# Four graph layers in one kernel: one activation table, powers on GpSimd, and relu slots shared by load

## The chip, the cores and the metric

The kernel runs on one core of a Trainium2 chip. Times are device microseconds (us) of one execution. Five engines matter: TensorE (PE, and PEld for its weight loads), VectorE (DVE), ScalarE (ACT), GpSimd (POOL) and the queue that starts transfers.

## The reference, cut to what matters

`x` is 64 batches of 256 nodes with 128 features; `adj` is one 256 x 256 matrix for all of them. Four pre-norm residual layers follow each other:

```python
h = relu(layernorm(x)); x = x + gated_steps(h, adj, 5)      # layer 0, five dependent steps:
#   m = adj @ h;  z = sigmoid(m @ w3' + h @ u3');  r = sigmoid(m @ w4' + h @ u3')
#   hv = tanh(m @ w5' + (r * h) @ u5');  h = (1 - z) * h + z * hv
h = relu(layernorm(x)); x = x + relu(chebyshev_hops(h, adj) @ Theta1 + bias)   # layer 1
h = relu(layernorm(x)); y = (adj @ h + h) @ weight + bias                       # layer 2
x = x + y / maximum(norm(y), 1e-12)
h = relu(layernorm(x))                                                          # layer 3
pre = s1[:, :, None, :] + s2[:, None, :, :] + b_lin      # [batch, i, j, e], e up to 256
e = (where(pre >= 0, pre, 0.2 * pre) * a).sum(-1) + adj
x = x + sigmoid(softmax(e, axis=2) @ h)
```

Layer 3 is the bulk: 256 x 256 x 256 leaky relus for each batch.

## The kernel before

Two batches (a pair) go through all layers together. Of leaky(p) = 0.2 p + 0.8 relu(p) the first part is separable; the second is made by VectorE and ScalarE, [128 e, 256 j] at a time, and summed over e by TensorE with a weight window of 32 columns. A *slot* is one relu tile: eight relus on one engine, then four 32-column products, one for each column group of the array. They run side by side: the four together take 0.86 us, and one alone took 0.97 (both from the trace, in the prediction). A pair has 128 slots.

```python
for r in range(32):
    for k in range(NE):
        rl = relu_pool.tile([P, 4, NB, N], F32, name="rl")        # 6 buffers
        on_act = turn[0] % 3 == 1                                  # every third slot on ScalarE
        turn[0] += 1
        for g in range(4):
            for b in range(NB):
                ...  # nc.scalar.activation(Relu) or nc.vector.tensor_scalar(add, max)
        for g in range(4):
            nc.tensor.matmul(flat[g * 32:(g + 1) * 32, :], win[:, k, 31 - r:63 - r], rl[:, g]...)
    background()          # after two slots: one stage of a softmax tail, one stage of the next pair's front
```

While layer 3 of pair p is worked off, `background()` emits the *front* (layers 0 to 2 and the projections) of pair p + 1. A front stage is mostly a full-width product on TensorE and the step of another engine that takes it out of its PSUM bank:

```python
pm = mix_nodes(h, adj_t, "pm"); mT = feat("mT"); nc.scalar.copy(mT, pm)
yield
pr = project([(w4t, mT), (u3t, hT)], "pr")
pz = project([(w3t, mT), (u3t, hT)], "pz")
nc.scalar.activation(r, pr, AF.Sigmoid, bias=br, scale=1.0)
nc.scalar.activation(z, pz, AF.Sigmoid, bias=bz, scale=1.0)
nc.vector.tensor_mul(rh, r, hT)
yield
pv = project([(w5t, mT), (u5t, rh)], "pv")
nc.scalar.activation(hv, pv, AF.Tanh, bias=bh, scale=1.0)
```

The norms take a square root on ScalarE, for which another activation table has to be loaded (125 of the trace's 285 table loads stand at the two lines of the roots), and a reciprocal on VectorE. The order in which one engine's instructions stand in its queue is decided when the program is built, by the framework's scheduler, from the order of emission and its own estimate of times; the engine then works its queue off in the order that was built.

Of the kernel before, what the change touches and what calls it, by code (L numbers as in the profile page):

```python
# [14 lines left out]
P = 128  # L15
NB = 2  # batches handled together: 512 tokens, one PSUM bank per [128, 512] product
# [3 lines left out]
ALPHA = 0.2  # L20


@with_exitstack
def kernel(
# [22 lines left out]
    """Four pre-norm residual graph layers over x [B, 256, 128].  # L47

    Every batch is independent, so a pair of batches goes through all four
    layers on chip. Token-major tiles are [token % 128, batch, token // 128,  # L50
    feature]; feature-major ones are [feature, batch, token].

    The last layer's scores sum a_e * leaky(s1[i, e] + s2[j, e]) over e. With
    leaky(p) = ALPHA * p + (1 - ALPHA) * relu(p) the first part is separable,
    and the second is relu on the vector and scalar engines (e on partitions,
    j along the free axis, s1[i] as the per-partition scalar), reduced over e
    by the tensor engine: a stationary [128, 32] window, zero but for one
    column that holds (1 - ALPHA) * a, puts row i into its place in PSUM.
    """
# [27 lines left out]
    ident = const.tile([P, P], F32, name="ident")  # L87
    make_identity(nc, ident)
    eps_t = const.tile([P, 1], F32, name="eps_t")
    nc.vector.memset(eps_t, LN_EPS)  # L90

    adj_n = const.tile([P, NC, N], F32, name="adj_n")  # [n, c, m]: adj[c * 128 + n, m]
    nc.sync.dma_start(adj_n, adj.rearrange("(c p) m -> p c m", p=P))
    adj_t = const.tile([P, NC, N], F32, name="adj_t")  # [m, c, n]: adj[n, c * 128 + m]
    adj_ti = const.tile([P, NC, N], F32, name="adj_ti")  # the same of adj + I
# [8 lines left out]
    def load_transposed(w, name):  # L104
        """w [128, D] or [128, 2 * D] -> its transpose, the halves summed (both multiply the same message)."""
        cols = w.shape[1]
        raw = work.tile([P, 2 * D], F32, name="w_raw", bufs=3)
        nc.scalar.dma_start(raw[:, :cols], w)
        src = raw[:, :D]
        if cols == 2 * D:  # L110
            s = work.tile([P, D], F32, name="w_sum")
            nc.vector.tensor_add(s, raw[:, :D], raw[:, D:])
            src = s
        pt = bank([P, P], "pt")
        nc.tensor.transpose(pt, src, ident)
        t = const.tile([P, P], F32, name=name)
        nc.vector.tensor_copy(t, pt)
        return t
# [5 lines left out]
    u5t = load_transposed(u5_w, "u5t")  # L124
# [5 lines left out]
    nc.vector.tensor_add(gate_b[:, 0:1], braw[:, 0:1], braw[:, 3:4])  # L130
    nc.vector.tensor_add(gate_b[:, 1:2], braw[:, 1:2], braw[:, 3:4])
    nc.vector.tensor_add(gate_b[:, 2:3], braw[:, 2:3], braw[:, 4:5])
# [18 lines left out]

    blin = const.tile([P, NE], F32, name="blin")
# [6 lines left out]
    a_lin = const.tile([P, NE, N], F32, name="a_lin")  # L159
    nc.vector.memset(a_lin, ALPHA)  # L160
    for k in range(NE):
        nc.vector.tensor_scalar(win[:, k, 31:32], acol[:, k:k + 1], 1.0 - ALPHA, None, op0=OP.mult)
        nc.vector.tensor_scalar(a_lin[:, k, :], a_lin[:, k, :], acol[:, k:k + 1], None, op0=OP.mult)

# [1 line left out]
    def norm_relu(src, h):  # L166
        """h = relu(layernorm(src)) over the features, token-major."""
# [7 lines left out]
        std = work.tile([P, NB * NC], F32, name="std")  # L175
        nc.scalar.activation(std, mv[:, :, 1], AF.Sqrt, bias=eps_t, scale=1.0)
        rstd = work.tile([P, NB * NC], F32, name="rstd")
        nc.vector.reciprocal(rstd, std)
        for k in range(NB * NC):
            nc.vector.tensor_scalar(hh[:, k, :], s[:, k, :], mv[:, k, 0:1], rstd[:, k:k + 1],  # L180
                                    op0=OP.subtract, op1=OP.mult)
        nc.vector.tensor_scalar(hh, hh, 0.0, None, op0=OP.max)

    def to_feature(h, name):
        """Token-major -> feature-major, in PSUM."""
# [6 lines left out]
    def to_token(ht, name):  # L192
        """Feature-major -> token-major, in PSUM."""
# [6 lines left out]
    def mix_nodes(h, a, name):  # L200
        """[f, b, n] = sum over nodes m of h[b, m, f] * a[m, n], in PSUM."""
# [6 lines left out]
    def project(pairs, name):  # L208
        """[o, b, n] = sum of w[f, o] * t[f, b, n] over the pairs (w, t), in PSUM."""
        pp = bank([P, NB, N], name)  # L210
        for k, (w, t) in enumerate(pairs):
            nc.tensor.matmul(pp.rearrange("p b n -> p (b n)"), w, t.rearrange("p b n -> p (b n)"),  # L212
                             start=(k == 0), stop=(k == len(pairs) - 1))
        return pp

    def project_token(pairs, name):
        """[n, b, c, o] = sum of t[f, b, n] * w[f, o] over the pairs (t, w), in PSUM."""
# [6 lines left out]
        return pp  # L224
# [6 lines left out]

    READY = {}

    def front(p):
        """Layers 0 to 2 of pair p and the operands of layer 3; yields between its stages."""
        x0 = XIN.pop(p)

        # layer 0: gated message passing
        h = tok("h")
        norm_relu(x0, h)  # L240
# [3 lines left out]
        nc.scalar.copy(hT, pt)  # L244
        yield
        for step in range(STEPS):
            pm = mix_nodes(h, adj_t, "pm")
            mT = feat("mT")
            nc.scalar.copy(mT, pm)  # L249
            yield  # L250
            pr = project([(w4t, mT), (u3t, hT)], "pr")
            pz = project([(w3t, mT), (u3t, hT)], "pz")
            r = feat("r")
            nc.scalar.activation(r, pr, AF.Sigmoid, bias=br, scale=1.0)  # L254
            z = feat("z")
            nc.scalar.activation(z, pz, AF.Sigmoid, bias=bz, scale=1.0)  # L256
            rh = feat("rh")
            nc.vector.tensor_mul(rh, r, hT)  # L258
            yield
            pv = project([(w5t, mT), (u5t, rh)], "pv")  # L260
            hv = feat("hv")
            nc.scalar.activation(hv, pv, AF.Tanh, bias=bh, scale=1.0)  # L262
            yield
            # (1 - z) * h + z * hv = h + z * (hv - h)
            nc.vector.tensor_sub(hv, hv, hT)  # L265
            nc.vector.tensor_mul(hv, hv, z)
            hT_new = feat("hT")
            nc.vector.tensor_add(hT_new, hT, hv)
# [3 lines left out]
            if step < STEPS - 1:  # L272
                h = tok("h")
                nc.scalar.copy(h, pt)  # L274
                yield
        x1 = tok("x1")
        nc.vector.tensor_add(x1, x0, pt)
        yield

        # layer 1: Chebyshev hops; both hop families use adj, so their weights are summed  # L280
        h = tok("h")
        norm_relu(x1, h)
# [3 lines left out]
        nc.scalar.copy(hT, pt)  # L286
        yield
        pm = mix_nodes(h, adj_n, "pm")
        c1T = feat("c1T")
        nc.scalar.copy(c1T, pm)  # L290
        yield
        pt = to_token(c1T, "pt")
        c1 = tok("c1")
        nc.scalar.copy(c1, pt)
        yield
        pm = mix_nodes(c1, adj_n, "pm")
        c2T = feat("c2T")
        nc.vector.scalar_tensor_tensor(c2T, pm, 2.0, hT, op0=OP.mult, op1=OP.subtract)
# [3 lines left out]
        for k in range(NB * NC):  # L302
            b, c = divmod(k, NC)
            nc.vector.tensor_add(y[:, b, c, :], po[:, b, c, :], bias1)
        x2 = tok("x2")
        nc.vector.scalar_tensor_tensor(x2, y, 0.0, x1, op0=OP.max, op1=OP.add)
        yield

        # layer 2: (adj + I) h W + bias, rows normalised
        h = tok("h")  # L310
        norm_relu(x2, h)
# [3 lines left out]
        nc.scalar.copy(yT, pm)  # L315
# [3 lines left out]
        for k in range(NB * NC):  # L319
            b, c = divmod(k, NC)  # L320
            nc.vector.tensor_add(y[:, b, c, :], po[:, b, c, :], bias2)
        yield
        sq = tok("sq")
        nc.vector.tensor_mul(sq, y, y)
        nrm = work.tile([P, NB, NC], F32, name="nrm")
        nc.vector.tensor_reduce(nrm, sq, AX.X, OP.add)
        nc.vector.tensor_scalar(nrm, nrm, NORM_EPS * NORM_EPS, None, op0=OP.max)
        nc.scalar.activation(nrm, nrm, AF.Sqrt)
        rn = work.tile([P, NB, NC], F32, name="rn")
        nc.vector.reciprocal(rn, nrm)  # L330
        x3 = tok("x3", bufs=3)
        for b in range(NB):
            for c in range(NC):
                nc.vector.scalar_tensor_tensor(x3[:, b, c, :], y[:, b, c, :], rn[:, b, c:c + 1], x2[:, b, c, :],
                                               op0=OP.mult, op1=OP.add)
        yield

        # layer 3: its input and the two projections by the halves of adj
        h3 = tok("h3", bufs=3)
        norm_relu(x3, h3)  # L340
        yield
        pt = to_feature(h3, "pt")
        hT = feat("hT")
        nc.scalar.copy(hT, pt)
        yield
        s1, s2 = [], []
        for k in range(NE):
            pa = project([(adj_t[:, 0, k * P:(k + 1) * P], hT)], "pa")
            t1 = feat(f"s1_{k}")
            nc.vector.tensor_scalar(t1, pa, blin[:, k:k + 1], None, op0=OP.add)  # L350
            pb = project([(adj_t[:, 1, k * P:(k + 1) * P], hT)], "pb")
            t2 = feat(f"s2_{k}")
            nc.scalar.copy(t2, pb)
# [3 lines left out]
        READY[p] = (x3, h3, s1, s2)  # L357

    def tail(p, ic, pe, x3, h3):
        """Softmax, the weighted sum and the output of rows ic * 128 ... of pair p."""  # L360
        t = work.tile([P, NB, N], F32, name="sc")
        for b in range(NB):
            nc.vector.tensor_add(t[:, b, :], pe[:, b, :], adj_n[:, ic, :])
        nmx = work.tile([P, NB], F32, name="nmx")
        nc.vector.tensor_reduce(nmx, t, AX.X, OP.max, negate=True)  # L365
# [73 lines left out]
    while fronts:  # L439
        step(fronts)  # L440
# [44 lines left out]
```

## Time and profile before

| | before |
|---|---|
| time, median of 3 | 7427.82 us (7427.02 to 7432.16) |
| TensorE, VectorE, ScalarE, GpSimd busy | 98, 92, 75, 0% |
| relus on VectorE / ScalarE | 21848 / 10920 |
| activation table loads | 285, 1283 ns each |
| the chain that ended last | TensorE 87%, VectorE 12% |

The page, the chain and the window sums are shown in the prediction. One more view is the waits (engine, line, what it waited for: us in total, times, longest us). Here are TensorE's weight loads and three of the waits of the relu producers:

```profile
PEld pe L421 <- DVE rl L417: 1569.0, 3674, 2.5
...
ACT rl L415 <- PE pe L421: 394.5, 447, 2.4
DVE rh L258 <- ACT r L254: 237.3, 51, 10.6
...
ACT mT L249 <- PE pm L205: 154.3, 108, 3.9
```

The first line is TensorE waiting for relus of VectorE (counted at its weight loads, which overlap the products before them, so not all of it is lost time). The second is ScalarE waiting for a relu buffer to come free: it has time over. The last two are steps of the front which wait until another engine is done.

### The profile page before, as it was taken

Reading aid. Unit: us, or ns where it says so; the run is one execution under the profiler, and the core shown is the slowest. Engines: PE = TensorE matmul, PEld = TensorE weight load, DVE = VectorE, ACT = ScalarE, POOL = GpSimd, SP = SyncE. Lnnn points to the kernel's source line nnn. Section 1 sums busy time; section 2 is a strip of 40 time slices with the busy share of each in tenths; the row PEclk is TensorE's granted clock in tenths of the full one; section 3 lists DMA queues with packets and bytes.
Section 4 is the critical chain, followed back from the end, with each engine's and each line's share of the span. In section 5 each row is a group of like instructions: output and inputs, shape, how many; then the busy total and the mean of one; then the engine's idle time right before and its main releaser. Section 6 shows DMA issues by size and latency. Waiting matters only on the chain.

```text
span 7427.2 us, 120750 instructions
## 1 busy us (share of the span) xinstructions
PE 7242.1 (98%) x40713; PEld 2490.1 (34%) x40713; DVE 6813.8 (92%) x25298; ACT 5601.2 (75%) x12837; POOL 0.7 (0%) x6
## 2 busy tenths in 40 slices
PE   6999999999999999999999999999999999999999
PEld 3333333333333333333333333333333333333333
DVE  4998999999999999998999999999989999999999
ACT  3777777778777777777777777777877777777777
POOL 0000000000000000000000000000000000000000
PEclk8999999999999999999999999999999999999999
DMA  0000000000000000000000000000000000000000
GB/s 13 3 4 4 3 2 3 4 4 3 2 4 3 4 3 2 4 3 4 4 3 3 3 4 4 3 2 4 3 4 3 2 4 3 4 2 2 2 2 3
DMA packets 38816, 25.83 MB, mean 3 GB/s; under 512 B 3504, under 2 KB 38192, under 8 KB 38192
## 3 DMA queue, kind: packets, MB, share of 16 engines
q1 hardware_dynamic: 35088, 17.05, 0.8%
q8 instruction: 319, 5.23, 0.3%
q14 instruction: 305, 2.50, 0.1%
q10 hardware_dynamic: 3104, 1.05, 0.1%
HBM read 9.70 MB, written 8.39 MB: 2 GB/s over the span
## 4 chain that ended last, share of the span: by engine, by line
PE 87%; DVE 12%; ACT 1%; issue 0%; DMA 0%; SPq 0%; ACTq 0%; DVEq 0%
PE pe L421 58%; PE pm L205 7%; DVE rl L417 6%; PE pr L212 4%; PE pz L212 4%; PE pv L212 4%; PE pe L403 2%; PE pe L399 2%; PE pt L197 2%; DVE h L180 1%; PE po L222 1%; PE po L381 1%; PE pa L212 1%; PE pb L212 1%; DVE stats L173 1%; PE pt L189 1%
## 5 line engine op out<-in xcount | busy, mean ns | idle before, releaser
L417 DVE TENSOR_SCALAR rl<-s,s 128x256 f32<-128x256 f32 x21848 | 5868.7, 347 | 46.8 <-PE pe L421 44.5
L421 PE MATMUL pe<-rl,win 128*32 128x512 f32 x32768 | 5102.9, 599 | 93.4 <-DVE rl L417 93.4
L415 ACT ACTIVATE rl<-s,s 128x256 f32<-128x256 f32 x10920 | 4531.2, 497 | 399.6 <-PE pe L421 394.5
L421 PEld LDWEIGHTS pe<-rl,win 128*32 128x32 f32 x32768 | 1295.7, 109 | 3162.2 <-DVE rl L417 1569.0
L205 PE MATMUL pm<-adj_t,h 128*128 128x256 f32 x1280 | 336.0, 400 | 2.8 <-ACT h L274 2.8
L258 DVE TENSOR_TENSOR rh<-r,hT 128x512 f32<-128x512 f32 x160 | 109.8, 686 | 237.9 <-ACT r L254 237.3
L205 PEld LDWEIGHTS pm<-adj_t,h 128*128 128x128 f32 x1280 | 232.4, 195 | 166.3 <-issue 78.0
L249 ACT COPY mT<-pm 128x512 f32<-128x512 f32 x160 | 93.7, 586 | 155.3 <-PE pm L205 154.3
L254 ACT ACTIVATE r<-pr,gate_b 128x512 f32<-128x512 f32 x160 | 109.9, 687 | 114.5 <-PE pr L212 114.5
L369 ACT ACTIVATE sc<-sc,nmx 128x256 f32<-128x256 f32 x128 | 64.5, 504 | 157.3 <-DVE nmx L365 156.8
L212 PE MATMUL pr<-mT,w4t 128*128 128x512 f32 x320 | 178.9, 641 | 3.5 <-ACT mT L249 3.5
L212 PE MATMUL pv<-mT,w5t 128*128 128x512 f32 x320 | 179.5, 643 | 0.0
L403 PE MATMUL pe<-a_lin,s 128*128 128x256 f32 x512 | 168.6, 419 | 0.0
L212 PE MATMUL pr<-hT,u3t 128*128 128x512 f32 x320 | 167.3, 604 | 0.0
L212 PE MATMUL pz<-mT,w3t 128*128 128x512 f32 x320 | 165.9, 600 | 0.0
L212 PE MATMUL pv<-rh,u5t 128*128 128x512 f32 x320 | 164.5, 595 | 0.0
L262 ACT ACTIVATE hv<-pv,gate_b 128x512 f32<-128x512 f32 x160 | 108.7, 680 | 73.1 <-PE pv L212 73.0
L212 PE MATMUL pz<-hT,u3t 128*128 128x512 f32 x320 | 163.4, 592 | 0.0
L256 ACT ACTIVATE z<-pz,gate_b 128x512 f32<-128x512 f32 x160 | 109.3, 683 | 64.8 <-PE pz L212 64.8
L265 DVE TENSOR_TENSOR hv<-hv,hT 128x512 f32<-128x512 f32 x160 | 109.7, 686 | 37.7 <-ACT hv L262 36.3
L403 PEld LDWEIGHTS pe<-a_lin,s 128*128 128x128 f32 x512 | 80.9, 188 | 181.4 <-issue 179.8
L399 PE MATMUL pe<-s,a_lin 128*128 128x512 f32 x256 | 141.1, 640 | 0.0
(108 smaller groups left out, 3577.9 us busy)
## 6 DMA issues: line engine op xcount, KB each, us to landing
xin<-in_x_dram SPq DMA_DIRECT2D x64, 128.0 KB, 2.2
out_dram<-o SPq DMA_DIRECT2D x64, 128.0 KB, 1.8
w_raw<-in_L_gnn_w_w_dram ACTq DMA_DIRECT2D x3, 128.0 KB, 2.6
th_raw<-in_L_gnn_Theta_dram ACTq DMA_DIRECT2D x1, 320.0 KB, 3.4
adj_n<-in_adj_dram SPq DMA_DIRECT2D x1, 256.0 KB, 4.7
w_raw<-in_L_gnn_u_w_dram ACTq DMA_DIRECT2D x2, 64.0 KB, 2.6
bias<-in_L_gnn_bias_dram ACTq DMA_DIRECT2D x2, 64.0 KB, 3.5
w<-in_L_gnn_weight_dram ACTq DMA_DIRECT2D x1, 64.0 KB, 3.1
```

The source lines that it names most:

```text
L197: nc.tensor.transpose(pt[:, b, c, :], ht[:, b, c * P:(c + 1) * P], ident)
L205: nc.tensor.matmul(pm[:, b, :], h[:, b, c, :], a[:, c, :], start=(c == 0), stop=(c == NC - 1))
L212: nc.tensor.matmul(pp.rearrange("p b n -> p (b n)"), w, t.rearrange("p b n -> p (b n)"), start=(k == 0), stop=(k == len(pairs) - 1))
L254: nc.scalar.activation(r, pr, AF.Sigmoid, bias=br, scale=1.0)
L256: nc.scalar.activation(z, pz, AF.Sigmoid, bias=bz, scale=1.0)
L258: nc.vector.tensor_mul(rh, r, hT)
L265: nc.vector.tensor_sub(hv, hv, hT)
L399: nc.tensor.matmul(flat, a_lin[:, k, :P], s2[k].rearrange("p b n -> p (b n)"), start=(k == 0), stop=False, skip_group_check=True)
L403: nc.tensor.matmul(pe[:, b, :], s1[k][:, b, ic * P:(ic + 1) * P], a_lin[:, k, :], start=False, stop=False, skip_group_check=True)
L415: nc.scalar.activation(rl[:, g, b, :], s2[k][:, b, :], AF.Relu, bias=sc, scale=1.0)
L417: nc.vector.tensor_scalar(rl[:, g, b, :], s2[k][:, b, :], sc, 0.0, op0=OP.add, op1=OP.max)
L421: nc.tensor.matmul(flat[g * 32:(g + 1) * 32, :], win[:, k, 31 - r:63 - r], rl[:, g].rearrange("p b n -> p (b n)"), start=False, stop=(r == ...
```

## The change

Its intent is to unload VectorE and to use ScalarE's free time: one activation table for all (sigmoid(x) = (1 + tanh(x/2))/2; roots as powers on GpSimd), so that table loads go; fewer products (r and z share a bank, the z weights being added as a difference; the separable scores as one product with a vector computed ahead; the second Chebyshev hop as one product with a matrix computed ahead); wider norm passes; each slot given to the engine with the smaller load so far; and a front stage after single slots, spread evenly over the pair. The core of the diff:

```diff
-        nc.scalar.activation(std, mv[:, :, 1], AF.Sqrt, bias=eps_t, scale=1.0)
-        nc.vector.reciprocal(rstd, std)
+        nc.gpsimd.tensor_scalar(dst, src, add, None, op0=OP.add)
+        nc.gpsimd.tensor_tensor(dst, dst, mhalf, op=OP.pow)      # and two stages until it is used
...
-            pr = project([(w4t, mT), (u3t, hT)], "pr")
-            pz = project([(w3t, mT), (u3t, hT)], "pz")
-            nc.scalar.activation(r, pr, AF.Sigmoid, bias=br, scale=1.0)
+            add_project(pg, [(u3t, hT), (w4t, mT)], True, True)
+            act_fn(r, pg, AF.Tanh, br, 0.5)
+            yield
+            add_project(pg, [(w34t, mT)], False, True)           # w34t = w3t - w4t, onto the same bank
...
-            for k in range(NE):      # separable scores: two products of s2, four of s1
-                nc.tensor.matmul(flat, a_lin[:, k, :P], s2[k]...)
-            ...
+            nc.tensor.matmul(pf, v_rep, hT..., start=True, stop=False)
...
-                    on_act = turn[0] % 3 == 1
+                    on_scalar = load["act"] + 8 * 399 < load["dve"] + 8 * 263
...
-                background()         # once per row, that is after two slots
+                    background()     # after each slot
...
-            step(pending)
-            step(fronts)
+            done[0] += 1
+            if done[0] % 4 == 2:
+                step(pending)
+            while fronts and done[1] * (SLOTS - 6) < done[0] * (stages + 1):
+                done[1] += 1
+                step(fronts)
```

## The prediction

> **What bounds the kernel now.** I read the page first (engines, chain of waits, costliest groups), then the chain in order of time inside one pair of batches, then the timeline of TensorE and of two relu stretches. The page:
>
> ```profile
> PE 7242.1 (98%) x40713; PEld 2490.1 (34%) x40713; DVE 6813.8 (92%) x25298; ACT 5601.2 (75%) x12837; POOL 0.7 (0%) x6
> PE 87%; DVE 12%; ACT 1%; issue 0%; DMA 0%; SPq 0%; ACTq 0%; DVEq 0%
> L417 DVE TENSOR_SCALAR rl<-s,s 128x256 f32<-128x256 f32 x21848 | 5868.7, 347 | 46.8 <-PE pe L421 44.5
> L421 PE MATMUL pe<-rl,win 128*32 128x512 f32 x32768 | 5102.9, 599 | 93.4 <-DVE rl L417 93.4
> L415 ACT ACTIVATE rl<-s,s 128x256 f32<-128x256 f32 x10920 | 4531.2, 497 | 399.6 <-PE pe L421 394.5
> ```
>
> Three engines share the relu slots of layer 3: 4096 slots, each of eight relus on VectorE or ScalarE and four 32-column matmuls (two records each) on TensorE. TensorE's 98% cannot be taken at its word, since its ends are modelled. So I price its work from the distance between starts in the chain (start us, us, what):
>
> ```profile
> 3057.22 53.43 PE pe L421 x326
> ...
> 3174.04 0.59 PE pt L197 x4
> 3174.63 1.85 PE pe L421 x16
> 3176.48 1.93 PE pm L205 x8
> 3178.41 1.85 PE pe L421 x16
> 3180.26 1.91 PE pr L212 x4
> 3182.18 1.72 PE pz L212 x4
> 3183.89 1.85 PE pe L421 x16
> 3185.75 1.91 PE pv L212 x4
> 3187.66 3.57 PE pe L421 x32
> ```
>
> Two regimes show. From 3174 on (a gate step of layer 0) one TensorE piece follows the next without a hole: TensorE sets the pace, 17.2 us a step. At 3057 there is nothing but relu slots: 326 records, 40.75 slots, take 53.43 us or 1.31 us a slot, where two slots take 1.85 us above. There the relu producers set the pace. Window sums confirm it (columns: span, then PE, PEld, DVE, ACT busy): VectorE is full in both, so the two engines are close to balance.
>
> ```profile
> 3056.00:3110.00 54.00, 54.00 (x329) 17.60 (x328) 54.00 (x207) 43.77 (x105) 0.00 (x0) 1.00 0.00 1
> 3140.00:3197.00 57.00, 57.00 (x354) 20.90 (x352) 56.95 (x202) 47.98 (x111) 0.00 (x0) 1.00 0.00 1
> ```
>
> Prices of TensorE: 16 relu records 1.85 = 2 x 0.86 + 0.13; 32 records 3.57 = 4 x 0.86 + 0.13. Full-width: four 512-column records 1.91 = 2 x 0.86 + 0.19; pm's eight 1.93 = 4 x 0.43 + 0.19; four transposes 0.59. So every change between narrow and full width costs 0.13 and 0.19 us. Worse is a broken group of four:
>
> ```profile
> 3110.58 1.12 PE L399 MATMUL pe<-s,a_lin 128*128 128x512 f32 x2
> 3111.64 1.04 PE L421 MATMUL pe<-rl,win 128*32 128x512 f32 x2
> 3112.61 1.13 PE L399 MATMUL pe<-s,a_lin 128*128 128x512 f32 x2
> ```
>
> One relu matmul between two full-width ones runs from 3111.64 to 3112.61, 0.97 us, as long as four together. Producers, from stretches without a wait:
>
> ```profile
> 3011.25 3.28 ACT L415 ACTIVATE rl<-s,s 128x256 f32<-128x256 f32 x8
> 3013.34 6.12 DVE L417 TENSOR_SCALAR rl<-s,s 128x256 f32<-128x256 f32 x23
> ```
>
> (3.28 - 0.50) / 7 = 0.40 us a relu on ScalarE, (6.12 - 0.35) / 22 = 0.262 on VectorE: 3.2 and 2.1 us a slot.
>
> **What the Trainium skill says.** "Perfetto Trace Analysis", Identifying the Most-Contended Engine, warns that matmul busy time is a bad measure; the trace agrees (98% busy, yet slots at 1.31 us in one stretch and 0.93 in another). "TensorEngine Tiling (Array Packing)", Key Properties: a change of tiling mode drains TensorE; the 0.13 and 0.19 us above agree. "ScalarE: Activation LUTs", What ACT_TABLE_LOAD costs: 1283 ns for each load, plus a drain; the trace has 285 loads at 1283 ns. "SBUF — State Buffer", SBUF: two separate sides: GpSimd and VectorE's two-port instructions lock one port pair against each other for a whole instruction; no run here shows it yet, as GpSimd is idle.
>
> **The change, part by part.** Counts come from the instruction order of the two built programs.
>
> VectorE. Relus 21848 to 19632: 2216 x 0.262 = 581 us less. Other work by cadence (mean less the 0.08 us by which neighbours overlap): before about 1050 us. Four norm pieces, the max and the reciprocal (0.26 x 4 + 0.33 + 0.09) become two 512-wide passes (0.60 x 2): 128 x 0.25 = 32 less. The 64 shifts of s1 go to ScalarE (42); the squares, their sum and small ops go (48); c2T goes (19); the bias adds become wide (12); the score add and max (81) become one fused op (about 56, an estimate), the doubled sums cost 5. Sum about 175 less. Busy: 6814 - 581 - 175 = about 6060.
>
> ScalarE. Out: 285 table loads but one (285 x 1.283 = 366), the roots (about 30) and one copy (15). In: 2216 relus x 0.40 = 886, shifts 37, c2T 15, 128 squares with their sums about 40 (estimate). 5601 - 411 + 978 = about 6170, less where records overlap; by cadence 5990. So the sharing by load brings both to about 6000 to 6100.
>
> TensorE. Out: one gate product a step (160 x 0.86 = 137), the score parts 128 x 0.86 + 256 x 0.43 = 220 against 64 x 0.86 = 55 (165), the transposes of c1T (14): 316 us less of full-width work (1921 to 1607). In: more breaks. The scheduler, now fed a stage at a time between single slots, cuts more finely: changes to full width 1567 to 2053, relu runs of one matmul 256 to 493. With groups priced as above, relu work goes from 3894 to 4285 us, and changes from 0.32 x 1567 = 502 to 0.32 x 2053 = 657. Sum: 1921 + 3894 + 502 = 6317 before, 1607 + 4285 + 657 = 6549 after. TensorE's demand rises by some 230 us although its products shrink: this is the step that I hold the gain to be decided by.
>
> The time. The front of a pair is now spread evenly over its 128 slots. Cut where layer 0 ends, a pair of the changed kernel has a gate part of 69 slots with 125 us of TensorE and a rest of 59 slots with 81 us. Producers: the time t in which both engines make S slots beside other work d and a obeys (t - d)/2.1 + (t - a)/3.2 = S. Gate part: d = 14, a = 15.5: 103 us, so TensorE sets it, 125 to 128. Rest: d = 13, a = 8: 86 us against 81, both near, so with waits in the norm chains 88 to 92. A pair: about 217. Before, the same cut gives TensorE 93 of 50 slots and 105 of 78 slots, the latter ruled by VectorE (52 slots x 2.1 + 19 = 128), sum 221 against a real 230, so 4% are lost to waits; I leave 2 to 3% in the 217, since the slow root chains get two stages of slack. 31 pairs x 217 = 6727; the opening, front of pair 0 alone, 135 as now (the first slots come after 120 to 140 us); the last pair without a front 128/0.79 = 165; the end 10. Sum 7037. With no loss at all in either part (125 + 86) it is 6850. I take a little under the middle of the two: 6950.
>
> What is not on the path: the 366 us of table loads. ScalarE had 1.8 ms of slack; they count only as room for 2216 relus.
>
> **Rivals.** (1) VectorE or ScalarE bound at the new balance: 6060 + opening and waits, some 6350 to 6500. For: VectorE is 92% busy and every part of the change unloads it. Against: the gate steps run on TensorE without a hole, and its demand after is 6549 before any wait. (2) Engines wait for each other in order: with all three within 8% there is no slack; a gate product must now wait until ScalarE has read the shared bank, and single relus between single products starve TensorE. Then a pair loses 10% and more: 7250 to 7500. For: VectorE now waits 237 us for ScalarE in rh (longest 10.6), where norm chains and loads pile up. Against: those loads are gone, and in the gate steps three engines ran at 100, 100 and 84% without a hole. (3) GpSimd's powers: 320 instructions. If each held the port for 1 us, VectorE would lose 320 us, most of it in the rest part, which VectorE rules: plus 150 to 250. If GpSimd in turn gets no port between VectorE's two-port relus, the roots come late and the norm waits: plus 1 to 2 us for each of 160 roots.
>
> **Range and chances.** 6950, down to 6750 if the producers keep TensorE fed throughout (near rival 1), up to 7200 if rivals 2 or 3 take 3% more. 2% below 7428 is 7279: faster 0.93, within 2% 0.06, slower 0.01.
>
> **What would show it.** Right: TensorE leads the chain with more than 80%; relu pieces of x2 to x14 beside full-width ones in nearly every stretch, no stretch of 50 us of relus alone; VectorE about 6060 and ScalarE about 6000 busy, both near 87%; a pair of about 215 us; one table load. Wrong: VectorE or ScalarE leading the chain (rival 1 where the time is under 6650, rival 2 where it is long with holes in all three); relus of VectorE longer than 0.262 us beside GpSimd's powers (rival 3); a relu run of one matmul much cheaper than 0.97 us.

## The result, and the profile after

The changed kernel takes 7433.01 us (median of 4 runs, 7431.12 to 7434.1), the kernel before 7427.42 (7421.91 to 7432.16) beside it. Ratios here and below are the mean time of one kernel's fast runs over that of the other's of the same rounds, so not quite the ratio of the medians quoted: 1.0007, with a 95% interval from 0.9992 to 1.0021. Nothing was gained.

The page after, the same lines as the prediction showed of before:

```profile
PE 7357.8 (99%) x39637; PEld 2268.8 (31%) x39637; DVE 6097.8 (82%) x22287; ACT 6083.8 (82%) x14929; POOL 582.4 (8%) x327
...
PE 94%; DVE 3%; POOL 1%; ACT 1%; issue 0%; DMA 0%; ACTq 0%; DVEq 0%
...
L486 PE MATMUL pe<-rl,win 128*32 128x512 f32 x32768 | 5481.2, 599 | 11.4 <-DVE rl L482 6.2
L480 ACT ACTIVATE rl<-s,s 128x256 f32<-128x256 f32 x13136 | 5359.1, 499 | 6.5 <-PE pe L486 6.1
L482 DVE TENSOR_SCALAR rl<-s,s 128x256 f32<-128x256 f32 x19632 | 5265.5, 345 | 61.2 <-PE pe L486 57.6
```

The work went where it was meant to: VectorE's busy time fell by 716 us, ScalarE took 2216 relus more and is still below 6100, and the relus are no slower (345 against 347 ns, 499 against 497). The chain is TensorE's, at 94%. Both producers are busy for 82% only, and yet the span is the same. The number to look at is in the third line: the same 16384 relu products (two records each) are on TensorE for 5481 us where they were for 5103.

TensorE's timeline (start us, us, engine, line, operation, shapes, how many) shows what such a stretch looks like:

```profile
3022.58 0.60 PE L253 MATMUL pm<-adj_n,h 128*128 128x256 f32 x2
...
3023.11 1.05 PE L486 MATMUL pe<-rl,win 128*32 128x512 f32 x2
...
3024.08 0.70 PE L253 MATMUL pm<-adj_n,h 128*128 128x256 f32 x2
```

One relu product (two records) stands between the halves of one front product. It takes from 3023.11 to 3024.08, 0.97 us, as long as four products which fill all four column groups (0.86 + 0.13). Such single products were 256 before and are 493 now, as the built order had said.

The waits after:

```profile
PEld pe L486 <- ACT rl L480: 1010.1, 2079, 1.2
PEld pe L486 <- DVE rl L482: 800.1, 2116, 1.9
...
DVE rh L316 <- ACT r L283: 423.5, 150, 8.6
...
DVE hv L327 <- ACT hv L283: 334.8, 152, 5.9
ACT mT L279 <- PE pm L253: 295.5, 135, 3.9
DVE y L362 <- PE po L268: 188.6, 32, 9.4
...
DVE rl L482 <- PE pe L486: 57.6, 59, 4.2
```

TensorE waits for relus of both engines, and at the same time both engines wait at front steps: VectorE for ScalarE's r (424 us, 237 before) and hv (335), ScalarE for the product that mT is copied from (296, 154 before). The idle time that the change was to buy is spent there. The last line is VectorE before a relu buffer that is not yet free. By the trace 61 of its 1329 idle us lie before relus, and of ScalarE's 1342 not even 10; nearly all the rest lies before steps of the front and of the softmax tail.

**An account of TensorE's time.** From the trace I take each run of relu products from its first start to the start of the next full-width piece, and set it against its price by the prediction's rule (0.86 for each started group of four, 0.858 before rounding, + 0.13). What it lasts beyond its price I call *hunger*: TensorE stands in a relu run and has no finished relu. (It could also be a front product at the end of the run that waits for its own input. In the changed kernel that is some 3 us: so little lies, beyond 1 us each, between the last relu record of a run and the front product after it.) Full-width pieces are taken as they last, with their changes of width. These sums, and the time until the first relu product, give the whole span but for the last few microseconds:

| kernel | until the first relu product | full-width | relu runs at their price | hunger | sum |
|---|---|---|---|---|---|
| before | 141 | 2156 | 4098 | 1025 | 7420 |
| after | 124 | 1944 | 4552 | 803 | 7423 |
| after less before | -17 | -212 | +454 | -222 | +3 |

So 451 us were saved, half of them hunger, and 454 us were lost in the cutting of relu runs, in which the groups of four are broken more often. Two questions follow: is the order on TensorE really what costs these 454 us, and why are 803 us of hunger left, with producers that are idle for 18%?

### The profile page after: what moved, and what is told of

Same layout as the page of the kernel before. It is cut to its first block, busy times and chain, and to the rows that moved or that the text cites. A ratio compares the mean times of both kernels' runs of the same rounds, so it can differ in the third digit from the quotient of the medians.

```text
span 7429.3 us, 117874 instructions
## 1 busy us (share of the span) xinstructions
PE 7357.8 (99%) x39637; PEld 2268.8 (31%) x39637; DVE 6097.8 (82%) x22287; ACT 6083.8 (82%) x14929; POOL 582.4 (8%) x327
## 4 chain that ended last, share of the span: by engine, by line
PE 94%; DVE 3%; POOL 1%; ACT 1%; issue 0%; DMA 0%; ACTq 0%; DVEq 0%
PE pe L486 67%; PE pm L253 8%; PE pg L259 7%; PE pv L259 4%; PE pt L245 2%; PE po L268 2%; PE po L448 1%; DVE rl L482 1%; PE pa L259 1%; PE pe L465 1%; PE pb L259 1%; PE pt L237 1%; POOL rn L208 1%; ACT rl L480 1%; POOL rn L209 1%; DVE stats L218 0%
## 5 line engine op out<-in xcount | busy, mean ns | idle before, releaser
L486 PE MATMUL pe<-rl,win 128*32 128x512 f32 x32768 | 5481.2, 599 | 11.4 <-DVE rl L482 6.2
L480 ACT ACTIVATE rl<-s,s 128x256 f32<-128x256 f32 x13136 | 5359.1, 499 | 6.5 <-PE pe L486 6.1
L482 DVE TENSOR_SCALAR rl<-s,s 128x256 f32<-128x256 f32 x19632 | 5265.5, 345 | 61.2 <-PE pe L486 57.6
L206 POOL TENSOR_SCALAR rstd<-mv 128x4 f32<-128x4 f32 x128 | 117.2, 915 | 6238.5 <-DVE mv L219 6238.5
L316 DVE SCALAR_TENSOR_TENSOR rh<-r,hT 128x512 f32<-128x512 f32 x160 | 110.8, 692 | 423.5 <-ACT r L283 423.5
L209 POOL TENSOR_TENSOR rstd<-rstd,mhalf 128x4 f32<-128x4 f32 x128 | 294.1, 2298 | 10.7
L283 ACT ACTIVATE r<-pg,gate_b 128x512 f32<-128x512 f32 x160 | 109.9, 687 | 184.2 <-PE pg L259 184.1
L259 PE MATMUL pg<-mT,w34t 128*128 128x512 f32 x320 | 178.0, 638 | 0.0
L259 PE MATMUL pg<-hT,u3t 128*128 128x512 f32 x320 | 177.1, 635 | 0.0
L259 PE MATMUL pg<-mT,w4t 128*128 128x512 f32 x320 | 176.4, 633 | 0.0
```

The lines of the kernel that those rows point to most:

```text
L206: nc.gpsimd.tensor_scalar(dst, src, add, None, op0=OP.add)
L209: nc.gpsimd.tensor_tensor(dst, dst, mhalf, op=OP.pow)
L259: nc.tensor.matmul(pp.rearrange("p b n -> p (b n)"), w, t.rearrange("p b n -> p (b n)"), start=(start and k == 0), stop=(stop and k == len ...
L283: nc.scalar.activation(dst, src, fn, bias=bias, scale=scale)
L316: nc.vector.scalar_tensor_tensor(rh, r, 1.0, hT, op0=OP.add, op1=OP.mult)
L480: nc.scalar.activation(rl[:, g, b, :], s2[k][:, b, :], AF.Relu, bias=sc, scale=1.0)
```

## The experiments

All kernels gave correct results unless said otherwise.

**1. TensorE in the order of the program text.** The change as it is, but the scheduler may not reorder TensorE's instructions; VectorE and ScalarE are ordered by it as before.

```diff
+    keep = ExitStack()
+    keep.enter_context(tc.manual_schedule(engines={mybir.EngineType.PE}))
     for _ in front(0):
     ...
+    keep.close()
```

> The changed kernel with TensorE alone held to the order in which the program emits its products; nothing else differs. The built order has 1184 full-width pieces in place of 2053 and no relu run that is not a multiple of four, so TensorE's demand, priced as in the prediction, is 5500 us in place of 6549. Theory A (the scheduler's cuts took the gain: broken groups of four and changes of width): VectorE and ScalarE (6100 us each) set the time, 6450 to 6750. Theory B (engines waiting for each other in order, mostly for ScalarE's slow slots, whatever TensorE's demand): 7150 or more. Theory C (GpSimd's powers): no change, 7430.

Measured: 6773.79 us (6771.9 to 6776.2), ratio 0.9118 (0.9105 to 0.9132). This is 9% faster than both kernels, just above theory A's range; B and C are out. The page and the waits:

```profile
PE 6701.5 (99%) x39637; PEld 2275.2 (34%) x39637; DVE 6091.6 (90%) x22287; ACT 6085.0 (90%) x14929; POOL 535.0 (8%) x327
...
L486 PE MATMUL pe<-rl,win 128*32 128x512 f32 x32768 | 4928.0, 599 | 12.7 <-ACT rl L480 8.4
```

```profile
PEld pe L486 <- ACT rl L480: 1173.5, 2284, 1.4
...
DVE rh L316 <- ACT r L283: 180.0, 128, 8.9
```

The same instructions, the same producers' busy time to 0.1%, and 659 us less. In the built order there are 1184 full-width segments for 2053, and TensorE's demand by the price rule is 5500 us for 6549. The wait of rh went from 424 to 180 us. (The order on VectorE and ScalarE is not quite the same: counted in the traces, each kind of front step stands on average up to 7 relus later than in the changed kernel, less than one slot.)

**2. A front stage after two slots again,** as before the change.

```diff
-                    background()
+                background()
...
-            done[0] += 1
-            if done[0] % 4 == 2:
-                step(pending)
-            while fronts and done[1] * (SLOTS - 6) < done[0] * (stages + 1):
-                done[1] += 1
-                step(fronts)
+            step(pending)
+            step(fronts)
```

> The changed kernel with one front stage and one tail stage after every row of two slots, as the kernel before has it; the front is bunched into the first part of a pair again. Demand of TensorE by the built order 6261 us (1818 full-width pieces). Theory A: demand falls by 288, but the bunched front leaves a relu stretch that the producers rule again, so 7150 to 7350. Theory B (waits from the thin spreading): 7000 or less if the spreading made them; unchanged if not.

Measured: 7244.01 us, ratio 0.9752 (0.9737 to 0.9766), in theory A's range. The built order has 1818 segments and a demand of 6261 us. So the finer spreading of the front and tail stages, which I took for a help, costs 189 us of the change.

**3. Nine relu buffers instead of six.**

```diff
-    relu_pool = ctx.enter_context(tc.tile_pool(name="relu", bufs=6))
+    relu_pool = ctx.enter_context(tc.tile_pool(name="relu", bufs=9))
```

> The changed kernel with nine relu buffers in place of six; the built order is the same. Theory A: less than 1 per cent faster (7360 to 7430), as more buffers take nothing off TensorE's demand. Theory B with buffers as the limit of running ahead: 3 to 6 per cent faster (7000 to 7200).

Measured: 7431.53 us, ratio 1.0003 (0.9986 to 1.002). The buffers limit nothing.

**4. Every third slot on ScalarE again,** as before the change.

```diff
-                    on_scalar = load["act"] + 8 * 399 < load["dve"] + 8 * 263
+                    on_scalar = turn[0] % 3 == 1
+                    turn[0] += 1
```

> The changed kernel with the fixed share of before (every third relu slot on ScalarE). VectorE's relus are 21848 again, its busy time about 6680; demand of TensorE by the built order 6803 us, as the scheduler cuts more (2532 pieces). Theory A: slower by 200 to 400 us, 7600 to 7850. Theory B with ScalarE's slow slots as the cause of TensorE's waits: equal or faster, 7250 to 7430.

Measured: 7820.05 us, ratio 1.0526 (1.051 to 1.0542). The order of TensorE changes too (2532 segments, demand 6803), so this is not the worth of the sharing alone; experiment 9 is cleaner.

**5. The kernel before with TensorE in the order of the program text,** the edit of experiment 1 in the kernel before.

> The kernel before, with TensorE alone held to emission order, as in the first experiment: demand of TensorE 5755 us in place of 6317 (999 full-width pieces, all relu runs multiples of four). Theory A (the cuts hid the change's gain): the producers' side now decides and VectorE's 6814 us of before is the bound, 7000 to 7200, so that in like order the changed kernel (6774) is 3 to 6 per cent faster than the kernel before. If emission order alone made the gain of the first experiment and the change is worth nothing, this run lands at 6700 to 6850.

Measured: 7204.02 us, ratio 0.9696 (0.968 to 0.9713), at the upper edge of what was expected. Its demand falls from 6317 to 5755, but:

```profile
PE 6746.5 (94%) x40713; PEld 2531.4 (35%) x40713; DVE 6818.8 (95%) x25298; ACT 5607.8 (78%) x12837; POOL 0.7 (0%) x6
...
PE 68%; DVE 28%; ACT 2%; issue 1%; DMA 0%; ACTq 0%; DVEq 0%
```

VectorE is now 95% busy and has 28% of the chain: it is close to being the bound. In like order of TensorE, the change is thus worth 6774 / 7204 = 0.940, 6%. One difference goes with it: the granted clock was 0.97 in all four executions of this kernel, against 0.996 in experiment 1. Its trace has TensorE at half clock for 459 us, in short stretches of nearly every pair, where the changed kernel has 53 us, nearly all of it in the opening. How much of the 6% this makes is not shown.

**6. The kernel before with one table only:** sigmoids as tanh, roots on GpSimd, nothing else.

```diff
-        nc.scalar.activation(std, mv[:, :, 1], AF.Sqrt, bias=eps_t, scale=1.0)
-        nc.vector.reciprocal(rstd, std)
+        nc.gpsimd.tensor_scalar(std, mv[:, :, 1], LN_EPS, None, op0=OP.add)
+        nc.gpsimd.tensor_tensor(rstd, std, mhalf, op=OP.pow)
...
-            nc.scalar.activation(r, pr, AF.Sigmoid, bias=br, scale=1.0)
+            nc.scalar.activation(r, pr, AF.Tanh, bias=br, scale=0.5)
```

> The kernel before with only the sigmoids as tanh and the roots as GpSimd powers: 284 table loads of 1283 ns (364 us of ScalarE) go; products, sharing and stages stay. TensorE's demand by the built order rises from 6317 to 6475, as the scheduler cuts otherwise (1782 pieces). Prediction's claim (loads are not on the path) with theory A: 7430 to 7600. If loads were on the path: 7060 to 7200.

Measured: 7788.3 us, ratio 1.0481 (1.0466 to 1.0497), slower than expected.

```profile
PE 7455.7 (96%) x40713; PEld 2495.1 (32%) x40713; DVE 6833.1 (88%) x25235; ACT 5175.9 (66%) x12393; POOL 238.0 (3%) x327
...
PE 84%; DVE 12%; POOL 3%; ACT 1%; issue 1%; DMA 0%; ACTq 0%; POOLq 0%; DVEq 0%
```

ScalarE is rid of 425 us and the time rises by 358 (7788 less 7430 beside it). The account (146 until the first relu product, 2239 full-width, 4215 relu runs, 1176 hunger) names the parts: 83 more for full-width pieces, 117 for relu runs (the scheduler cut anew), 151 of hunger. GpSimd has 3% of the chain: without the two stages of slack that the change gives a root, it comes late (VectorE waits 193 us for it). TensorE was at half clock for 222 us, against 70 in the kernel before. So this run changes the order on TensorE and the roots along with the table loads, and can't price the loads alone; it shows only that to take them out in this way gained nothing. Experiment 9 is the better hint.

**7. All three engines in the order of the program text.**

```diff
-    keep.enter_context(tc.manual_schedule(engines={mybir.EngineType.PE}))
+    keep.enter_context(tc.manual_schedule(engines={mybir.EngineType.PE, mybir.EngineType.DVE, mybir.EngineType.Activation}))
```

> The changed kernel with TensorE, VectorE and ScalarE all in emission order; TensorE's order is that of the first experiment, 5500 us of demand. If the scheduler's order on the producers makes the waits that are left in the first experiment (6774 against 6090 busy on each producer): 6450 to 6650. If it hides latencies there, emission order makes it slower: 6850 to 7100.

Measured: 9734.4 us, ratio 1.3102 (1.3083 to 1.3122), far from both ranges.

```profile
PEld pe L486 <- ACT rl L480: 3457.9, 4409, 2.5
...
DVE rh L316 <- ACT r L283: 1259.2, 160, 13.5
...
ACT mT L279 <- PE pm L253: 563.4, 160, 5.0
```

In the text each step stands right behind the product that it needs. A producer then waits at nearly every front step (160 waits for 160 instructions of rh) and TensorE starves. So the scheduler helps on VectorE and ScalarE, where it puts relus ahead of a step that would wait (the gate steps of VectorE and ScalarE stand some 7 to 10 relus, about one slot, earlier here than in experiment 1, whose order of TensorE is the same instruction for instruction), and harms on TensorE alone. The order there must be asked engine by engine.

**8. Experiment 1 with half of the relus,** a wrong kernel on purpose (each relu tile is used for two column groups, TensorE's instructions are unchanged). One look, state unknown. The comparison with the reference let its result pass all the same.

```diff
-                    for g in range(4):
+                    for g in range(2):
...
-                                         rl[:, g].rearrange("p b n -> p (b n)"),
+                                         rl[:, g % 2].rearrange("p b n -> p (b n)"),
```

> A wrong result on purpose: the first experiment with each slot making two of its four relu pieces and each piece read twice, so the producers' work on relus halves and TensorE's program is the same, product for product. If the pricing of TensorE holds (5500 us of demand for this order): 5500 plus the opening's 70 us without work and a few waits, 5550 to 5800. If TensorE is not at its limit at the priced demand: 5300 or less; if waits in order cost TensorE whatever the producers do: 6200 or more.

Measured: 5618.17 us. With the producers at 64 and 65%, the hunger is 33 us, and the price rule (5500 from the built order, and an opening of 131) is right to within 1%:

```profile
PE 5554.2 (99%) x39637; PEld 1993.2 (35%) x39637; DVE 3608.8 (64%) x12471; ACT 3625.8 (65%) x8361; POOL 301.8 (5%) x327
...
PE 98%; DVE 1%; POOL 0%; ACT 0%; issue 0%; DMA 0%; ACTq 0%; DVEq 0%
```

**9. Experiment 1 with every third slot on ScalarE** (the diff of experiment 4 on top of experiment 1).

> The first experiment (TensorE in emission order, 6774) with the fixed share of before, every third slot on ScalarE. TensorE's program and demand are the same, 5500 us; VectorE is busy 6680 again. If in uncut order the sharing by load is what the change is worth: 7100 to 7250, close to the kernel before in emission order (7204). If the gain lies in the removed products and passes: 6800 to 6950.

Measured: 7107.79 us, ratio 0.9566 (0.955 to 0.9582). Of the 430 us between experiments 5 and 1, sharing by load is thus worth 334, taken as the last step, and all the rest of the change 96; the 96 include the table loads and the lower clock of experiment 5. The first branch of what was expected came true.

**10. Experiment 1 without the powers on GpSimd,** wrong (relative error 0.36): a constant made by one small VectorE operation takes the root's place.

```diff
-        nc.gpsimd.tensor_scalar(dst, src, add, None, op0=OP.add)
-        ...
-        nc.gpsimd.tensor_tensor(dst, dst, mhalf, op=OP.pow)
+        nc.vector.tensor_scalar(dst, src, 0.0, 1.0 if add is not None else 0.05, op0=OP.mult, op1=OP.add)
```

> A wrong result on purpose: the first experiment with each root replaced by one VectorE instruction that writes a constant, so GpSimd does nothing in the loop. If GpSimd's powers matter, by the shared port or by their 2 to 4 us each: 6774 less 2 to 5 per cent, 6450 to 6640. If not (VectorE waits for GpSimd for 22 us in all in the changed kernel): 6720 to 6800.

Measured: 6762.43 us, ratio 0.9103 (0.9089 to 0.9116): 11 us. GpSimd, its port and its late roots are no cause here.

**11. Experiment 1 with a stage between each front product and the step that takes it out** (ten more yields of this kind, and the product of the z weights moved behind rh):

```diff
             pg = bank([P, NB, N], "pg")
             add_project(pg, [(u3t, hT), (w4t, mT)], True, True)
+            yield
             r = feat("r")
             act_fn(r, pg, AF.Tanh, br, 0.5)
```

> The first experiment with one more stage boundary between each product of the front and the instruction that takes it out of PSUM, so that producers come to it later; demand 5520 us. Theory: the 10 per cent in which both producers stand still are their waits in order for products of the front (rh, hv, mT, y, yT). Then these waits fall and the time is 6400 to 6650. If the waits are not what sets the time, or the boundaries only lengthen the chain: 6750 or more.

Measured: 6774.32 us, ratio 0.9118 (0.9104 to 0.9131), no change. It doesn't refute that such waits matter, though: it hardly moved them. The wait of rh is 196 us where experiment 1 has 180, as the scheduler still places the steps of VectorE and ScalarE by itself. It did place them otherwise, most of them 5 to 37 relus later, and the time stayed: a shift of this size, in this direction, was worth nothing.

**12. Experiment 1 with nine relu buffers** (the diff of experiment 3 on top of it).

> The kernel of the first experiment (the change, TensorE in the order in which the program was written, 6774 us) with nine instead of six buffers for the relu tiles. What holds the last 10 per cent of both producers there is open: TensorE waits 1173 us for ScalarE's relus and the pricing of its demand (5500) lies far below its time. If the producers stand still because all six relu buffers are full while TensorE works on front products, three more let them run ahead by half a load and the time falls to 6550 to 6720. If the two producers are simply uneven within a load, or their front steps come in bursts that six tiles can't level and nine can't either, it stays within 1 per cent of 6774.

Measured: 6774.09 us, ratio 0.9119 (0.9104 to 0.9135), no change: the second branch of what was expected.

By now I had counted, from the traces, how far the producers are ahead: every 0.5 us, finished relus less relu products begun, in slots.

| kernel | median lead | share of time at 4 slots or more |
|---|---|---|
| before | 1.75 | 8% |
| after | 1.62 | 0% |
| experiment 1 | 1.62 | 1% |
| experiment 12, nine buffers | 1.62 | 1% |
| experiment 8, half the relus | 4.25 | 68% |

In the changed kernel the buffers are seldom all taken: the wait of 58 us shown above is all that VectorE loses by them. Nine buffers (experiment 3) took that wait away, and the time stayed. Something else stops the producers first. The candidate: a producer soon comes, in its own queue, to a front step whose product stands in TensorE's queue behind relu products not yet begun. It can be ahead of TensorE by no more than that. The next two kernels take away these waits.

**13. Experiment 1, and 14. the changed kernel, with front steps that do not read their product.** Wrong (relative error 0.98): the steps of ScalarE and VectorE in the front, and the copy of the softmax weights, read a constant tile. TensorE issues all its products as before; the built demand is 5500 us in the one (as in experiment 1) and 6540 in the other (6549 in the changed kernel).

```diff
+    still = const.tile([P, NB * N], F32, name="still")
...
-        nc.scalar.copy(dst, src)
+        nc.scalar.copy(shape, still)
...
-        nc.scalar.activation(dst, src, fn, bias=bias, scale=scale)
+        nc.scalar.activation(dst.rearrange("p b n -> p (b n)"), still, fn, bias=bias, scale=scale)
...  # likewise x1 <- pt and the two y <- po on VectorE
```

> Wrong result on purpose. The first experiment's kernel (the change with TensorE in the order in which the program was written, 6774 us) with all front steps of ScalarE and VectorE reading a constant tile instead of the bank that a front product of TensorE filled; the products are still issued, and wait for their inputs as before. TensorE's priced demand is unchanged (5500 us by the built order). In the traces the producers are only a median of 1.6 slots ahead of TensorE, though six buffers would allow more, and with half the relus (where nothing starves) 4.1. Theory A: in its own program order a producer soon comes to a front step whose product stands in TensorE's queue behind the relu products, so it can never be far ahead and TensorE starves at each uneven stretch. Then the lead grows to 4 slots or more, the hunger of some 1190 us falls by more than half, and the time comes down to what the producers' 6090 us and the opening allow: 6250 to 6450. Theory B: the shares are uneven within a few slots, or the buffers and semaphores cost it, and the front's waits are a symptom: 6680 to 6800.

> Wrong result on purpose. The changed kernel itself, order left to the scheduler, with the same edit: front steps read a constant tile, not the bank of TensorE. The built order prices TensorE at 6540 us, against 6549 for the changed kernel, so only the waits differ. Theory A (the waits of the producers for front products make TensorE's hunger of some 800 us, the term that the prediction took at about 400 with the opening): 6540 plus an opening of some 120 plus a small rest, 6680 to 6950. Theory B (they are a symptom; the hunger is made by uneven shares): 7300 to 7450.

Measured: 6155.8 us (0.8284, 0.8271 to 0.8296) and 6877.78 us (0.9255, 0.924 to 0.9271). B is out in both. The first is even below A's range, the second within it. The page of 13, then the page of 14:

```profile
PE 6131.5 (100%) x39637; PEld 2171.9 (35%) x39637; DVE 6040.7 (98%) x22288; ACT 6043.9 (98%) x14929; POOL 589.8 (10%) x327
```

```profile
PE 6825.9 (99%) x39637; PEld 2110.2 (31%) x39637; DVE 6079.6 (88%) x22288; ACT 6080.3 (88%) x14929; POOL 528.5 (8%) x327
```

The order on TensorE is the same: in 13 instruction for instruction, in 14 by its price. On VectorE and ScalarE it is not, since a step that waits for nothing may be placed elsewhere. Counted in the traces of 14 and the changed kernel, the gate steps stand on average 4 to 12 relus earlier, and pieces that now depend on little (the later layers, their norms, y) some 30 to 950. So the two kernels take away the waits and move the steps, and how much of the gain is the moving is not shown. Against it stands experiment 11, where a move changed nothing, and experiment 7, where the gate steps stand a slot earlier with their waits in place and the time is 9734 us. The producers' busy time is the same within 1% (the copies are no faster from the constant tile: 607 ns for mT in 14, 583 in the changed kernel), so what went are waits. In the changed kernel's order the waits now fall to the other side, as they should where TensorE is the bound. In the waits of 14 both producers stand before a relu buffer that is not yet free:

```profile
ACT rl L484 <- PE pe L490: 759.8, 447, 6.4
...
DVE rl L486 <- PE pe L490: 566.5, 377, 5.2
```

The account, with the two kernels that they stand against:

| kernel | until the first relu product | full-width | relu runs at their price | hunger | median lead, slots |
|---|---|---|---|---|---|
| experiment 1 | 131 | 1777 | 3668 | 1192 | 1.62 |
| 13 | 66 | 1777 | 3668 | 637 | 2.0 |
| after | 124 | 1944 | 4552 | 803 | 1.62 |
| 14 | 67 | 1941 | 4545 | 318 | 3.1 |

TensorE's own work is the same within 10 us in each couple. Hunger falls by 555 and 485 us, and the opening, in which the front of the first pair runs alone, by 65 and 57. One part of A was wrong: the lead grows to 3.1 slots in 14 but only to 2.0 in 13. There both producers are 98% busy, which means they are the bound, and what they finish is used at once; the 637 us of hunger that remain there are a sign of full producers.

## Why the prediction was wrong, point by point

The prediction said 6950 (6750 to 7200); the kernel takes 7433.

- **What the work of VectorE and ScalarE becomes: right.** 6060 and about 6000 were predicted for their busy time; 6098 and 6084 are measured (82% of the longer span, not 87). One table load, relus as long as before beside GpSimd's powers, TensorE with 94% of the chain: all as said.
- **The price of single relu products: right.** 0.976 us on average, over the 256 of the kernel before and over the 493 after; experiment 8 runs at the price of its order.
- **The rise of TensorE's demand by 230 us: right.** The account has 6254 before and 6496 after (full-width and relu runs), +242. Experiments 1, 2 and 5 show that the order does it, with the same products in each: 6774 and 7244 against 7433, and 7204 against 7427.
- **The table loads off the path: nothing speaks against it, but it isn't shown alone.** ScalarE had 1% of the chain before. In experiment 6, 425 us less on ScalarE bought nothing, but other costs came with it; in experiment 9 against 5 all of the change but the sharing, loads included, was worth 96 us.
- **The failing step: "I leave 2 to 3% in the 217, since the slow root chains get two stages of slack".** Together with its opening, this step left about 400 us (6950 less 6549) for everything that is not TensorE's demand. The account has 803 of hunger and 124 of opening, and the end. By pairs: without loss it is 125 + 86 = 211 us; 217 was predicted, 230.0 measured (mean of 31 pairs, counted in the trace by their relu products), which is a loss of 9%. The first 69 slots took 132.2 us where 125 to 128 was said, the other 59 took 97.8 where it was 88 to 92. The 13 us above the prediction, times 31 pairs, are 403 of the 483 us missed; most of the rest is the step from the worked sum of 7037 down to 6950. The roots were the wrong thing to look at: VectorE waits for them for only some 22 us in all. What ties the producers are their waits for front products and for each other. Where these waits are gone, in experiment 14, a pair takes 214.1 us (123.2 and 90.9), as the prediction's sum had it, and the kernel 6878. The prediction had in effect left these waits out.
- **Small slips in its sums, which decide nothing.** 128/0.79 is 162, not 165 (166.6 was measured); the gate part's equation gives 102 us, not 103; and 6950 lies a little above the middle of 6850 and 7037, not under it.
- **Rival 2 was the one that came,** in size (7250 to 7500, a pair losing 9% where it said 10) and in that engines wait for each other in order. Its detail that TensorE waits for the shared bank is not borne out: the front's products hardly wait (the 3 us of the account, and full-width pieces of 1944 us where their price, 1607 + 0.19 x 2053, is 1997). It was put aside because "in the gate steps three engines ran at 100, 100 and 84% without a hole". That was one stretch of the kernel before; it said nothing about a kernel in which both producers have a fifth of their time free and spend it at front steps, waiting for TensorE's queue and for each other.
- **Rival 1 is what the work allows.** Experiment 13, which is a wrong kernel but has all instructions of the change, takes 6156 us with both producers at 98%, even less than the rival's 6350. Rival 3 fell: 11 us (experiment 10, in experiment 1's order).

So the expected gain went into two places: 454 us into relu runs that the finer emission made the scheduler cut more often, which the prediction had priced; and some 500 us of waits which it had not, and which producers with time to spare did not make vanish. The first is shown by experiment 1. For the second, the idle time before front steps is seen in the trace, and experiment 14 shows that without these waits, and with the steps moved, most of the loss is gone. What stays open is how the two parts of experiment 14 share it, and how to be rid of the waits in a correct kernel. Each front step depends on the one before, and two more kernels that tried (11 and 12, both in experiment 1's order) moved nothing; giving the front of two pairs side by side to the queues was not tried.

The version that beats both kernels is experiment 1, at 6774 us.

## What to carry to other kernels

Where a scheduler fills one engine's queue from two streams, count how often it switches between them and price the switches before and after; take the engine's order as a thing to set by hand, engine by engine, as here a few lines turned a rewrite that gave nothing into one that gives 9%. An engine that is not busy is not therefore ahead: look at how many of its buffers are ever full. Here the producers' own queues held steps that waited for their consumer, and more buffers did not let them run ahead. And where a busy time falls while the span stays, look for a wait that has not been found yet: replace what the waiting steps read by a constant, and the difference is about its price. Then compare the order of the instructions in both traces too, as a scheduler may move what no longer waits.

## What the Trainium skill lacked or had wrong

- "TensorEngine Tiling (Array Packing)", Key Properties, says that changing the tiling mode drains TensorE, and traces agree; it has no figure. Here a change cost 0.13 us from 32-column to full-width products and 0.19 us back, and a single 32-column product between two full-width ones took 0.97 us, as long as four of them side by side. In this kernel, relu runs priced so come to 454 us more after the change than before.
- "SBUF — State Buffer", SBUF: two separate sides, led me to a rival in which VectorE loses up to 250 us to the port pair that it shares with GpSimd. With 160 powers and the 160 operations ahead of them on GpSimd, VectorE's relus took 345 ns against 347 without, and without GpSimd's work the kernel was 11 us (0.2%) faster. The page isn't wrong; instructions as small as 128 x 4 don't show it, and that VectorE's relus use both ports, as the rival had it, no run here shows either.
- "GPSIMD Engine Reference", Elementwise — side-by-side cycle accounting, has no power operation. On 128 x 4 elements it took 2298 ns on average for the norms and 3473 ns for the row norms, and the add or maximum ahead of it 915 and 1854 ns:

```profile
L206 POOL TENSOR_SCALAR rstd<-mv 128x4 f32<-128x4 f32 x128 | 117.2, 915 | 6238.5 <-DVE mv L219 6238.5
...
L209 POOL TENSOR_TENSOR rstd<-rstd,mhalf 128x4 f32<-128x4 f32 x128 | 294.1, 2298 | 10.7
```

- No page has the point that producers whose queues, kept in order, hold steps that wait for their consumer can't run ahead of it. Their median lead was 1.6 slots with six buffers and with nine, and 3.1 where those steps did not wait (experiment 14).
